# Keeping the slot masks of a graph kernel in DRAM, dropping a small store, moving a product to ScalarE, and smaller first batches

## The chip, the cores and the metric

The kernel runs on one core of a Trainium2 chip. The metric is the time of one execution on the device in microseconds (us). TensorE is called PE in the profile, VectorE DVE, ScalarE ACT, GpSimd POOL, SyncE SP. Transfers issued by SP stand in a queue of SP's own, which issues them in order; a transfer whose condition is not met holds up all behind it. [...]

## What is computed

Two graph layers over 6,250 nodes and 100,000 edges with 128 features each; the edges are sorted by their target node `dst`. Each layer is added to its input and normalized. Cut to what matters:

```python
# layer 0: two graph convolutions
deg  = segment_sum(ew, dst)                    # self-loops included
dinv = where(deg > 0, rsqrt(deg), 0)
h    = relu(segment_sum((x @ W1)[src] * norm[:, None], dst) + b1)
h    = segment_sum((h @ W2)[src] * norm[:, None], dst) + b2
x    = layernorm(x + sigmoid(h))
# layer 1: attention over the edges of a node
z  = x @ fc_w.T;  rh = edge_attr @ fc_r_w.T
e  = z[src] @ a0 + z[dst] @ a1 + rh @ a2
e  = where(e >= 0, e, 0.01 * e)
alpha = softmax of e over the edges of each dst
agg   = segment_sum(alpha[:, None] * (z[src] + rh), dst)
x  = layernorm(x + relu(agg + z @ loop_w))
```

## The kernel before

**Chunks and slots.** The edges are cut into 49 chunks (`NC`) of 2,048 (`CC`), each held as 128 partitions by 16 (`TC`). Since the edges are sorted by target, the targets of one chunk lie in a window of 144 nodes. The rows of the sources are gathered by matrix products with one-hot masks: the node table lies in SBUF as bf16 parts (`hot`), and each edge is given a slot, a group of 17 (`G`: 12 ordinary ones and 5 for spilled edges) and a place of 128 in that group. `sort()` (lines 688 to 787) works this out for three, then four, then seven chunks at a time: it ranks the edges, gets each edge's place `pm` and group `pg`, builds the two one-hot masks of a chunk, `ohm` (128x2048, place) and `ohg` (128x272, group), and brings the edges' data into slot order by the products of line 771. The slots' sources go to `srd` in DRAM, and from there come back spread over all partitions as `mask` rows (L849), are compared (L853) and stored for the later stages (`masks`, L854). The steps of `sort()` are dealt out between the chunks of the first convolution by `sort_to`.

**A chunk of a convolution.** `pick` (L467) gathers: 144 small products L476 into three PSUM tiles, copied with the slot's weight `swt` by ScalarE to `got` (L481), and five indirect loads by GpSimd for the spilled edges (`far`, L485). It builds the window mask `wm` on VectorE (L491, L498). `weigh` (L515) puts the weights on the spilled part of `wm` on ScalarE, `scatter` (L522) sums into the window on PE, and `add_in` (L527) adds the window to the accumulator. Scatter and addition of a chunk run one chunk later than its gather.

**The stages.** First convolution (L840 to L879), second convolution (L894 on, its order written out by hand), in which the attention scores of nodes `asd` are also worked out piece by piece with the layer's new node table (`x1_of`, L372; its bf16 parts are stored to `hz`, L426). Then comes the softmax stage (L1029 on), in which this change has most of its lines.

**The hand-over.** After the second convolution `asd` is stored to DRAM (L1019); only the branch for unusual graphs at the program's end reads that table, and it writes it itself first (L1407). Then `asd` is cut into bf16 parts `adp` (L1020 to L1023). `hot` is filled again from `hz` in four loads on ScalarE's queue (L1190).

**The softmax stage.** `scores()` (L1173) goes through batches of chunks: `ends` (scores of targets), `starts` (scores of sources, two halves per chunk: a row `rk` of 256 KB loaded on SP three ahead, L1054; compared on VectorE, L1087; 24 products L1094; `sel`, L1097; `asr`, L1098) and `softmax`. A chunk can only be summed once its batch is in `ready`. The batches hold 2, 5, then 7 chunks. While a batch is summed, the scores of the next are dealt out by `beside`. For each chunk, `shares` (L1196) brings the shares `al` to slot order: it builds `ohm` and `ohg` a second time (L1199, L1201) out of `pm` and `pg`, which stay in SBUF, multiplies (`put`, L1204), and sums in 16 products (L1208) and a reduction to `swt` (L1209). Then come `pick` and `scatter` as above, and `edge_part` (L1211): the edge features `et` are loaded in two halves (L1220), `ms` compares 16 segments with a window of 32 (L1225) and is multiplied by the shares `aw` (L1227), 16 products give `r` (L1238), ScalarE copies it (`sw`, L1243) and two products bring it to the window (L1249). `out_of` (L428) finishes blocks of nodes whose sums are complete.

**What sets the order.** Except in the second convolution, a scheduler sets the order of each engine's instructions and of each queue's transfers before the run, by its own estimate of when each is ready and by priority, which follows the order of the program text. Tiles come from pools with a set number of buffers (`bufs`); a tile's next use waits until the last reader of that buffer is done.

Of the kernel before, what the change touches and what calls it, by code (L numbers as in the profile page):

```python
# [10 lines left out]
BF16 = mybir.dt.bfloat16  # L11
I32 = mybir.dt.int32
AF = mybir.ActivationFunctionType
# [25 lines left out]
def gnn_kernel(ctx, tc, x, src, dst, ea, ew, W1, b1, W2, b2, fcw, fcrw, attn, loopw, out):  # L39
# [30 lines left out]
    while c0 < NC:  # L70
        n = min((2, 5)[len(batches)] if len(batches) < 2 else 7, NC - c0)
        batches.append((c0, n))
        c0 += n
# [31 lines left out]
    masks = dram.tile([NC, P, GP * P], BF16, name="masks")  # L105

# [82 lines left out]

    pm = keep.tile([P, NC, TC], BF16, name="pm")  # L190
    pg = keep.tile([P, NC, TC], BF16, name="pg")
# [495 lines left out]

    def sort():

        for c0, n in sorts:  # L690
# [61 lines left out]
            nc.vector.tensor_add(pm[:, some, :], r_, t_)  # L752
            nc.vector.scalar_tensor_tensor(t_, k_i[:, :n, :], float(GP), grp[:, some, :], op0=OP.add, op1=OP.subtract)
            nc.vector.tensor_mul(t_, t_, o)
            nc.vector.tensor_add(pg[:, some, :], grp[:, some, :], t_)
            slots = sp.tile([P, BATCH, NF], F32, name="slots")
            for c in cs:
                ohm = sp.tile([P, P, TC], BF16, name="ohm")
                nc.vector.tensor_tensor(ohm, iota_t, pm[:, c, None, :].to_broadcast([P, P, TC]), op=OP.is_equal)  # L759
                ohg = sp.tile([P, TC, G], BF16, name="ohg")  # L760
                nc.vector.tensor_tensor(ohg, iotab[:, None, :G].to_broadcast([P, TC, G]),
                                        pg[:, c, :, None].to_broadcast([P, TC, G]), op=OP.is_equal)
                put = sp.tile([P, TC, NF], BF16, name="put")
                nc.vector.tensor_tensor(put[:, :, : G * F].rearrange("p t (g f) -> p t g f", f=F),  # L764
                                        ohg[:, :, :, None].to_broadcast([P, TC, G, F]),
                                        rec[:, c, :, None, :].to_broadcast([P, TC, G, F]), op=OP.mult)
                nc.vector.tensor_tensor(put[:, :, G * F :], ohg[:, :, GP:],  # L767
                                        blk[:, c, :, None].to_broadcast([P, TC, GS]), op=OP.mult)
                ps = ps_c.tile([P, NF], F32, name="rec")
                for t in range(TC):  # L770
                    nc.tensor.matmul(ps, ohm[:, :, t], put[:, t, :], start=t == 0, stop=t == TC - 1)  # L771
                nc.scalar.copy(slots[:, c - c0, :], ps)
                yield
# [120 lines left out]
    with tc.tile_pool(name="conv2", bufs=2) as wp, tc.tile_pool(name="arp", bufs=2) as ap_, \  # L894
# [124 lines left out]
        nc.sync.dma_start(asd_d[:, :].rearrange("(b p) k -> p b k", p=P), asd)  # L1019
# [9 lines left out]
    with tc.tile_pool(name="look", bufs=2) as lp, tc.tile_pool(name="conv3", bufs=2) as wp, \  # L1029
# [20 lines left out]
        def sources(i):  # L1050

            if i < 2 * NC:
                rks[i] = lp.tile([P, HC], BF16, name="rk", bufs=3)
                nc.sync.dma_start(rks[i], srow[i // 2, None, i % 2 * HC : (i % 2 + 1) * HC].to_broadcast([P, HC]))  # L1054
# [129 lines left out]
        for i in range(2):  # L1184
            sources(i)
        steps = scores()
        next(steps)
# [7 lines left out]

        def shares(c, al3, i):  # L1196

            ohm = mp.tile([P, P, TC], BF16, name="ohm", bufs=1)
            nc.vector.tensor_tensor(ohm, iota_t, pm[:, c, None, :].to_broadcast([P, P, TC]), op=OP.is_equal)  # L1199
            ohg = mp.tile([P, TC, G], BF16, name="ohg", bufs=1)  # L1200
            nc.vector.tensor_tensor(ohg, iotab[:, None, :G].to_broadcast([P, TC, G]),  # L1201
                                    pg[:, c, :, None].to_broadcast([P, TC, G]), op=OP.is_equal)
# [8 lines left out]
        def edge_part(c, aw, i):  # L1211
# [15 lines left out]
            nc.vector.tensor_mul(ms, ms, aw[:, i, :, None].to_broadcast([P, NL, WS]))  # L1227
# [24 lines left out]
        pieces = Pieces(lambda b0, n: out_of(acc2, sum_r, b0, n, xp, ps_c, "rec"))  # L1252
        held = None
# [214 lines left out]
```

## Time and profile before

| | us |
|---|---|
| median of 3 runs | 2010.08 (2000.15 to 2014.5) |
| profiled execution | 2011.72, of which the span 2009.9 |
| first convolution, 49 chunks | 170 to 655 |
| second convolution, 49 chunks | 740 to 1205 |
| first batch ready in the softmax stage | about 1307 |
| `sw` copies of chunks 7, 35, 48 | 1438, 1847, 1985 |
| busy: PE, DVE, ACT, POOL | 1594.6, 1635.5, 945.4, 1102.0 |
| DMA: bytes, mean rate | 306.95 MB, 153 GB/s |

A row of the profile names the line, the engine, the operation, the written and the read tile, the count, and then the busy time and the mean duration in ns, followed by the idle time in front of such instructions and what ended it. Durations of neighbours on one engine overlap a little, so that a merged entry of twelve `got` takes 3.21 us though the mean of one is 0.38. "SPq" and "ACTq" rows are transfers being issued; their time is that of the issue, not of the transfer. A timeline row can merge neighbours of one kind ("x4").

### The profile page before, as it was taken

The page shows a single profiled execution, that of the slowest core. Times are in us where ns is not written, and L with a number is a line of the kernel's source. Part 1 is how long each engine was busy: PE and PEld are TensorE (multiplying, and loading weights), DVE is VectorE, ACT ScalarE, POOL GpSimd, SP SyncE. Part 2 cuts the span into 40 slices and gives each one's busy share as a digit, 9 for nine tenths or more (in the row PEclk, how much of TensorE's full clock was granted, in tenths as well). Part 3 has the DMA queues.
Part 4 walks back from the last instruction along what each step waited for, and adds up shares of the span by engine and source line. Part 5 has one row for each costly group of instructions (what it writes and reads, how often), then busy time and mean ns, then how long its engine had stood idle before and what let it go on. Part 6 is the DMA issues. An engine that isn't in the chain of part 4 may idle for free.

```text
span 2009.9 us, 78721 instructions
## 1 busy us (share of the span) xinstructions
PE 1594.6 (79%) x33767; PEld 1441.6 (72%) x33767; DVE 1635.5 (81%) x3252; ACT 945.4 (47%) x3098; POOL 1102.0 (55%) x953
## 2 busy tenths in 40 slices
PE   2877889988888868889888863368888888888996
PEld 2556878878877757778778752358877787877985
DVE  7787978988985348999989954689989999997773
ACT  1255445455455655577666743013433444434543
POOL 4026666777767348888888850214343434534772
PEclk9978989999999758899999985569999999999998
DMA  2115234244236247777777766655666666655662
GB/s 62 37 43 157 65 112 135 68 120 143 74 104 191 62 132 228 220 226 260 233 226 258 221 212 64 160 137 140 186 161 194 178 177 180 182 171 150 190 181 70
DMA packets 260881, 306.95 MB, mean 153 GB/s; under 512 B 44145, under 2 KB 199543, under 8 KB 253470
## 3 DMA queue, kind: packets, MB, share of 16 engines
q1 hardware_dynamic: 228915, 244.95, 40.0%
q0 software_dynamic: 23520, 48.22, 11.5%
q10 hardware_dynamic: 8088, 8.65, 1.4%
q8 instruction: 268, 4.39, 0.9%
q14 instruction: 90, 0.74, 0.1%
HBM read 260.42 MB, written 41.30 MB: 150 GB/s over the span
## 4 chain that ended last, share of the span: by engine, by line
PE 36%; DVE 36%; DMA 13%; issue 7%; ACT 6%; DVEq 1%; POOL 1%; SPq 0%; ACTq 0%; POOLq 0%
PE win L522 15%; PE g L476 7%; DVE wm L491 5%; DVE sel L1097 3%; DVE put L764 2%; DMA et<-in_edge_attr_dram 2%; DVE ohm L759 2%; PE rec L1208 2%; DVE et L980 2%; ACT got L481 2%; PE mm L333 2%; DMA mask<-srd 2%; DMA far<-g,sidx 2%; DMA mask<-masks 1%; DMA hz<-part 1%
## 5 line engine op out<-in xcount | busy, mean ns | idle before, releaser
L485 POOL DMA_INDIRECT far<-g,sidx x490 | 728.5, 1487 | 232.6 <-PE win L522 103.5
L481 ACT ACTIVATE got<-g,swt 128x128 f32<-128x128 f32 x1764 | 485.0, 382 | 373.5 <-PE g L476 170.3
L485 POOL DMA_INDIRECT far<-zd,sidx x245 | 309.9, 1265 | 459.0 <-PE win L522 332.3
L522 PE MATMUL win<-wm,got 128*128 128x144 f32 x3528 | 521.9, 305 | 11.6 <-issue 11.5
L522 PEld LDWEIGHTS win<-wm,got 128*128 128x128 f32 x3528 | 485.1, 204 | 29.4 <-issue 18.7
L476 PE MATMUL g<-hot,mask 128*32 128x128 bf16 x21168 | 392.8, 229 | 95.5 <-issue 55.3
L476 PEld LDWEIGHTS <-mask 128*32 128x32 bf16 x21168 | 336.3, 102 | 129.6 <-issue 93.2
L491 DVE TENSOR_TENSOR wm<-iota,sdst 128x1728 f32<-128x1728 f32 x147 | 286.7, 1950 | 3.9 <-DMA g<-rows 3.7
L515 ACT ACTIVATE wm<-wm,swt 128x64 f32<-128x64 f32 (+1 forms) x735 | 201.4, 356 | 80.6 <-DVE wm L498 46.2
L522 PE MATMUL win<-wm,far 128*128 128x64 f32 (+1 forms) x1470 | 187.0, 273 | 15.5 <-DMA far<-g,sidx 14.9
L522 PEld LDWEIGHTS win<-wm,far 128*128 128x128 f32 x1470 | 182.4, 194 | 16.9 <-issue 13.5
L1094 PE MATMUL k<-adp,rk 128*128 128x49 bf16 x2352 | 93.6, 196 | 64.5 <-DVE sel L1097 51.3
L1094 PEld LDWEIGHTS <-rk 128*128 128x128 bf16 x2352 | 86.0, 104 | 76.7 <-DVE rk L1087 40.9
L980 DVE TENSOR_TENSOR et<-et,ar_row 128x2048 f32<-128x2048 f32 (+1 forms) x49 | 111.6, 2279 | 25.9 <-DMA et<-in_edge_attr_dram 25.9
L527 DVE TENSOR_TENSOR acc<-acc,win 128x144 f32 x147 | 44.3, 302 | 99.4 <-PE win L522 86.8
L981 DVE TENSOR_REDUCE dots<-et 128x16 f32<-128x2048 f32 (+1 forms) x49 | 112.0, 2286 | 1.7
L322 POOL TENSOR_TENSOR hot<-low,hot 128x512 bf16<-128x512 f32 x24 | 32.5, 1355 | 141.1 <-DVE hot L321 101.6
L1097 DVE TENSOR_TENSOR sel<-k,ohb 128x392 f32<-128x392 f32 x98 | 84.0, 858 | 4.9 <-PE k L1094 4.6
L764 DVE TENSOR_TENSOR put<-ohg,rec 128x1360 bf16<-128x1360 bf16 x49 | 76.8, 1568 | 0.0
L717 ACT CAST own<-r 128x768 bf16<-128x768 f32 x49 | 39.3, 803 | 71.7 <-PE r L714 46.2
L771 PE MATMUL rec<-put,ohm 128*128 128x90 bf16 x784 | 59.1, 242 | 15.8 <-DVE put L767 14.9
L1087 DVE TENSOR_SCALAR rk<-rk,iotap 128x1024 bf16<-128x1024 bf16 x98 | 50.1, 511 | 26.5 <-DMA rk<-srow 26.5
(397 smaller groups left out, 2326.4 us busy)
## 6 DMA issues: line engine op xcount, KB each, us to landing
et<-in_edge_attr_dram SPq DMA_DIRECT2D x97, 512.0 KB
et<-in_edge_attr_dram SPq DMA_DIRECT2D x48, 1024.0 KB
mask<-masks SPq DMA_DIRECT2D x98, 384.0 KB
rk<-srow SPq DMA_DIRECT2D x98, 256.0 KB
mask<-srd SPq DMA_DIRECT2D x49, 384.0 KB
masks<-mask SPq DMA_DIRECT2D x49, 384.0 KB
far<-g,sidx POOLq DMA_INDIRECT x490
g<-rows SPq DMA_DIRECT2D x24, 256.0 KB
```

Source lines behind the costliest of these rows:

```text
L476: nc.tensor.matmul(ps[32 * q : 32 * q + 32, g, :], mask[:, (g0 + g) * P + 32 * q : (g0 + g) * P + 32 * q + 32], hot[:, 4 * (g0 + g) + q, k ...
L481: nc.scalar.activation(got[:, g, :], ps[:, g, :], AF.Copy, scale=swt[:, c, g0 + g : g0 + g + 1])
L485: nc.gpsimd.indirect_dma_start(out=got, out_offset=None, in_=table[:, :], in_offset=bass.IndirectOffsetOnAxis(ap=sidx[:, c, g : g + 1], ax ...
L491: nc.vector.tensor_tensor(wm[:, : GP * WC].rearrange("p (g w) -> p g w", w=WC), iota[:, None, 1 : WC + 1].to_broadcast([P, GP, WC]), sdst[ ...
L515: nc.scalar.activation(m, m, AF.Copy, scale=swt[:, c, g : g + 1])
L522: nc.tensor.matmul(ps[:, n0 : n0 + m.shape[-1]], rows[g], m, start=g == 0, stop=g == G - 1)
L764: nc.vector.tensor_tensor(put[:, :, : G * F].rearrange("p t (g f) -> p t g f", f=F), ohg[:, :, :, None].to_broadcast([P, TC, G, F]), rec[: ...
L771: nc.tensor.matmul(ps, ohm[:, :, t], put[:, t, :], start=t == 0, stop=t == TC - 1)
L980: nc.vector.tensor_mul(et[:n], et[:n], ar_row[:n, None, :].to_broadcast([n, TC, D]))
L981: nc.vector.tensor_reduce(dots[:n, c, :], et[:n], AX.X, OP.add)
L1094: nc.tensor.matmul(ps[:, s, :], mk[:, s * P : (s + 1) * P], adp[:, 0, k, :NB], start=k == 0, stop=k == 2)
L1097: nc.vector.tensor_mul(sel, ps, ohb.rearrange("p b s -> p s b"))
```

## The change

Six edits. The store of `asd` (old L1019) is left out. The first two `rk` rows and the first step of the scores are put under `tc.high_priority()`, so that the scheduler takes them ahead of others. `ohm` and `ohg` become the two parts of one tile `slot` (128 x 2,320 bf16), which `sort()` stores to the new DRAM table `slotd` as soon as it is built; `pm` and `pg` are now small tiles of the sort. In the softmax stage `shares` no longer builds the masks but takes them from a tile that was loaded from `slotd` (two buffers); it asks for the next chunk's at its start, and `load_slots(0)` stands before the loop. In `edge_part` the product of `ms` and `aw` becomes 16 activations on ScalarE, each 128x32 with the share as its scale. The batches hold 2, 3, 4, 5, then 7 chunks, nine in all where there were eight.

```diff
-        n = min((2, 5)[len(batches)] if len(batches) < 2 else 7, NC - c0)
+        n = min((2, 3, 4, 5)[len(batches)] if len(batches) < 4 else 7, NC - c0)
...
+    slotd = dram.tile([NC, P, P * TC + TC * G], BF16, name="slotd")
...
-    pm = keep.tile([P, NC, TC], BF16, name="pm")
-    pg = keep.tile([P, NC, TC], BF16, name="pg")
...
+    def slot_views(slot):
+        return (slot[:, : P * TC].rearrange("p (q t) -> p q t", t=TC),
+                slot[:, P * TC :].rearrange("p (t g) -> p t g", g=G))
...
-                ohm = sp.tile([P, P, TC], BF16, name="ohm")
-                nc.vector.tensor_tensor(ohm, iota_t, pm[:, c, None, :].to_broadcast([P, P, TC]), op=OP.is_equal)
-                ohg = sp.tile([P, TC, G], BF16, name="ohg")
+                slot = sp.tile([P, P * TC + TC * G], BF16, name="slot")
+                ohm, ohg = slot_views(slot)
+                nc.vector.tensor_tensor(ohm, iota_t, pm[:, c - c0, None, :].to_broadcast([P, P, TC]), op=OP.is_equal)
                 nc.vector.tensor_tensor(ohg, iotab[:, None, :G].to_broadcast([P, TC, G]),
-                                        pg[:, c, :, None].to_broadcast([P, TC, G]), op=OP.is_equal)
+                                        pg[:, c - c0, :, None].to_broadcast([P, TC, G]), op=OP.is_equal)
+                nc.sync.dma_start(slotd[c], slot)
...
-        nc.sync.dma_start(asd_d[:, :].rearrange("(b p) k -> p b k", p=P), asd)
...
-        for i in range(2):
-            sources(i)
-        steps = scores()
-        next(steps)
+        with tc.high_priority():
+            for i in range(2):
+                sources(i)
+            steps = scores()
+            next(steps)
...
+        slots_in = {}
+
+        def load_slots(c):
+            if c < NC:
+                slots_in[c] = mp.tile([P, P * TC + TC * G], BF16, name="slot", bufs=2)
+                nc.sync.dma_start(slots_in[c], slotd[c])
+
         def shares(c, al3, i):
-            ohm = mp.tile([P, P, TC], BF16, name="ohm", bufs=1)
-            nc.vector.tensor_tensor(ohm, iota_t, pm[:, c, None, :].to_broadcast([P, P, TC]), op=OP.is_equal)
-            ohg = mp.tile([P, TC, G], BF16, name="ohg", bufs=1)
-            nc.vector.tensor_tensor(ohg, iotab[:, None, :G].to_broadcast([P, TC, G]),
-                                    pg[:, c, :, None].to_broadcast([P, TC, G]), op=OP.is_equal)
+            ohm, ohg = slot_views(slots_in.pop(c))
+            load_slots(c + 1)
...
-            nc.vector.tensor_mul(ms, ms, aw[:, i, :, None].to_broadcast([P, NL, WS]))
+            for s in range(k):
+                nc.scalar.activation(ms[:, s, :], ms[:, s, :], AF.Copy, scale=aw[:, i, s : s + 1])
...
+        load_slots(0)
```

More of the change, by code (lines that the diff above doesn't have):

```diff
@@ L751, in sort @@
             nc.vector.tensor_mul(t_, t_, o)
-            nc.vector.tensor_add(pm[:, some, :], r_, t_)
+            pm = sp.tile([P, BATCH, TC], BF16, name="pm")
+            pg = sp.tile([P, BATCH, TC], BF16, name="pg")
+            nc.vector.tensor_add(pm[:, :n, :], r_, t_)
             nc.vector.scalar_tensor_tensor(t_, k_i[:, :n, :], float(GP), grp[:, some, :], op0=OP.add, op1=OP.subtract)
             nc.vector.tensor_mul(t_, t_, o)
-            nc.vector.tensor_add(pg[:, some, :], grp[:, some, :], t_)
+            nc.vector.tensor_add(pg[:, :n, :], grp[:, some, :], t_)
             slots = sp.tile([P, BATCH, NF], F32, name="slots")
             for c in cs:
-                ohm = sp.tile([P, P, TC], BF16, name="ohm")
-                nc.vector.tensor_tensor(ohm, iota_t, pm[:, c, None, :].to_broadcast([P, P, TC]), op=OP.is_equal)
-                ohg = sp.tile([P, TC, G], BF16, name="ohg")
+                slot = sp.tile([P, P * TC + TC * G], BF16, name="slot")
+                ohm, ohg = slot_views(slot)
+                nc.vector.tensor_tensor(ohm, iota_t, pm[:, c - c0, None, :].to_broadcast([P, P, TC]), op=OP.is_equal)
                 nc.vector.tensor_tensor(ohg, iotab[:, None, :G].to_broadcast([P, TC, G]),
-                                        pg[:, c, :, None].to_broadcast([P, TC, G]), op=OP.is_equal)
+                                        pg[:, c - c0, :, None].to_broadcast([P, TC, G]), op=OP.is_equal)
+                nc.sync.dma_start(slotd[c], slot)
                 put = sp.tile([P, TC, NF], BF16, name="put")
```

## The prediction

> **What bounds the kernel now.** I read the page's row of slices first, then the busy time by stages, then the timelines of the places where an engine stands idle. The stages are my cut: the first convolution (170 to 655 us), the second (740 to 1205), the hand-over to the softmax stage (1240 to 1310), that stage's first chunks (to 1438), its steady part (chunks 7 to 35) and its tail, where no scores are left to work out.
>
> ```profile
> DVE  7787978988985348999989954689989999997773
> ```
>
> VectorE (DVE) is at nine tenths for most of the span; the dips lie at 650 to 750 us and at 1205 to 1300. Busy time by stage (columns: stretch, length, then busy us and instructions of PE, PEld, DVE, ACT, POOL, granted clock, DMA share, GB/s):
>
> ```profile
> 170.00:655.00 485.00, 418.75 (x9258) 385.35 (x9260) 404.95 (x851) 249.81 (x862) 341.39 (x237) 0.93 0.41 120
> ...
> 1240.00:1310.00 70.00, 25.02 (x481) 22.38 (x480) 44.34 (x108) 3.74 (x10) 15.95 (x12) 0.51 0.86 128
> 1310.00:1438.00 128.00, 100.00 (x2226) 91.08 (x2227) 115.67 (x317) 40.59 (x148) 39.13 (x32) 0.84 0.56 147
> 1438.00:1847.00 409.00, 350.29 (x8150) 321.26 (x8154) 376.40 (x882) 165.15 (x559) 169.72 (x141) 0.96 0.63 175
> 1860.00:1985.00 125.00, 116.17 (x2816) 110.67 (x2805) 88.19 (x165) 64.56 (x233) 83.14 (x58) 1.00 0.65 173
> ```
>
> In the steady part DVE is busy 376.4 of 409 us (92%), TensorE (PE) 86%: DVE binds, PE is close behind. In the tail PE is at 93% and DVE at 71%: PE binds. One chunk takes 409/28 = 14.6 us in the first and 125/12 = 10.4 us in the second. In the hand-over nobody is busy. Its queue and DVE:
>
> ```profile
> 1238.82 0.37 SPq L1019 DMA_DIRECT2D asd_d<-asd  x1
> 1240.10 12.45 SPq L426 DMA_DIRECT2D hz<-part  x1
> ...
> 1255.56 5.84 SPq L1054 DMA_DIRECT2D rk<-srow  x1
> ```
> ```profile
> 1247.12 0.20 DVE L1078 TENSOR_TENSOR adg<-one,adg 128x48 f32<-128x48 f32 x1
> 1268.62 3.47 DVE L1087 TENSOR_SCALAR rk<-rk,iotap 128x1024 bf16<-128x1024 bf16 x1 [21.31 <-DMA rk<-srow]
> ```
>
> The store of the scores (L1019) is 49 x 128 = 6,272 pieces of 8 bytes. The next DMA behind it, a 96 KB store, needs 12.45 us only to be issued where its like takes 0.33; all that follows on that queue is late, and DVE waits 21.31 us for one row of `rk`. The durations that the sum needs, from the steady part:
>
> ```profile
> L481 ACT ACTIVATE got<-g,swt 128x128 f32<-128x128 f32 x336 | 93.1, 383 | 160.6 <-DVE swt L1209 111.8 <-PE win L522 39.1 <-DVE near L1073 5.4
> ...
> L1097 DVE TENSOR_TENSOR sel<-k,ohb 128x392 f32<-128x392 f32 x61 | 52.9, 868 | 1.4 <-PE k L1094 1.3
> ...
> L1199 DVE TENSOR_TENSOR ohm<-iota_t,pm 128x2048 bf16<-128x2048 bf16 x29 | 35.2, 1214 | 0.0
> ...
> L1227 DVE TENSOR_TENSOR ms<-ms,aw 128x512 f32<-128x512 f32 x28 | 18.9, 676 | 0.0
> ...
> L1201 DVE TENSOR_TENSOR ohg<-iotab,pg 128x272 bf16<-128x272 bf16 x30 | 13.0, 433 | 0.0
> ```
>
> **The change, part by part.** The profiled execution took 2011.7 us (span 2009.9 and 1.8 around it), 1.6 above the median of the runs, 2010.1.
>
> *The store goes.* What it held up is the 21.3 us wait and the stretched `rk` comparison behind it (3.47 us against the usual 0.48): 24.3 us at most. Next late are the transfers themselves: the last quarter of `hot` (1152 KB, landed 11.2 us after its issue at 1266.0 in the chain of waits), and the first two slot masks, which the new order puts among the `rk` rows on SP's queue. Each is 128 x 2,320 bf16 = 594 KB. I take 4 us off for that: **-20** (bounds -24 and -12). That the first `rk` rows and `dk` go ahead saves nothing more: the wait is for the fourth row, whose buffer is only free when PE has used the first, and until 1240 DVE waits for the chain of x1 pieces in any case. The place of L1037/L1038 behind them is free for the same reason.
>
> *Slot masks are loaded, not rebuilt; shares are multiplied on ScalarE.* DVE loses 1.214 + 0.433 + 0.676 = 2.32 us per chunk, 114 us in 49 chunks. What that is worth differs by stage.
> In the first chunks (0 to 6) DVE is at 90%: 7 x 2.32 x 0.9 = 14.6 us. The new batches ask scores of three chunks, not five, before chunk 2: four halves less by the fourth chunk in the new order, each 0.87 + 0.56 + 0.48 + 0.36 = 2.3 us, 9 us put off to where DVE has room. I take **-15** for both together (-24 to -8), since the first batch's softmax, whose chain is unchanged, still stands in front. The ninth softmax costs DVE some 8 us (its 25 small operations by their rows), under PE where DVE is no longer the bound; with that cover gone it is +8.
> In the steady part DVE comes to 13.4 - 2.3 = 11.1 us per chunk and PE, 350.3/28 = 12.5 us, binds. Filled as in the tail (93%) that is 13.45 us, or -32 in 28 chunks.
>
> ScalarE now bounds how well PE can be filled. The nearest row is the weighting of `wm`, also in place with a scale per partition, 128x64:
>
> ```profile
> 1874.78 0.35 ACT L515 ACTIVATE wm<-wm,swt 128x64 f32<-128x64 f32 x1 [3.88 <-DVE swt L1209]
> 1875.15 1.14 ACT L481 ACTIVATE got<-g,swt 128x128 f32<-128x128 f32 x4
> 1876.17 1.07 ACT L515 ACTIVATE wm<-wm,swt 128x64 f32<-128x64 f32 x4
> ```
>
> Four in 1.07 us, one alone 0.35: one every 0.24. The Trainium skill, "ScalarE: Activation LUTs", section "Rules for kernel authors", says to give a multiplication to VectorE, not to ScalarE, and its section on the cost of ACT_TABLE_LOAD gives 186 ns, 93 more for a scale held per partition, 0.833 ns per element, 93 ns of it overlapped: 0.213 us for 32 elements, 3.4 us for 16, where DVE took 0.68. By the row it is at most 16 x 0.24 = 3.8. I take 3.4, as these are half as wide. The rule alone would call this edit a loss of 2.7 us per chunk; the rows say that ScalarE had 8.7 us free per chunk in the steady part (5.9 busy of 14.6), so total time is no bound: 9.3 of 13.5, and 8.8 of 10.4 in the tail.
> Its order is. The new order on ScalarE in the tail is per chunk: 3 `wm`, 4 `got`, 14 `ms`, 8 `got`, 2 `ms`, 2 `wm`, `sw`. Behind the fourteen stand the last eight `got`, and the last two `ms`, for which the `r` products wait, and after them `sw`, L1249, the next one-hot products L1208 and `swt`, for which the next `wm` and `got` wait. That is a ring: `r` 1.1, `sw` with its hand-offs 0.8, L1249 0.8, L1208 1.2, `swt` 0.4, then 0.8 + 1.1 + 3.0 + 2.15 + 0.6 on ScalarE: 11.9 us, against 10.4 in the tail. Hand-offs are estimated from gaps of 0.2 to 0.3 in the timeline, so I take 11.5: **+13** in 12 chunks (0 to +18). In the steady part `sel` and `k` work adds about a microsecond and a half to the ring, 13.4, about PE's 13.45; the two will not mesh fully: 13.8, **-22** (-32 to 0).
>
> *Storing the masks in the first convolution.* 49 stores of 594 KB. In order, SP has seven stores in a row, then the `srd` store and the mask rows; the rows needed `srd` before too, so nothing new queues there except until the seventh comparison is done, which `srd` also needs. What is new: the comparison for chunk c+2 waits until the store of c has landed. In the trace the two pairs are built from 360.19, both `ohg` done at 365.80, and the third `ohm` starts at 369.64: 3.8 us. The Trainium skill, "DMA: Bandwidth & Descriptors", "Anatomy of one DMA", fits 2.0 us plus bytes/436e3: 3.4 us, no wait. By the trace, 1152 KB in 11.2 us amid traffic, it is 5.8: 2 us for each of 8 bursts, 16. The bursts fall into lulls of DMA (share 0.41 in the stage), so I am near the first: 4. Also, the first slot store is now ahead of the `degr` load on SP, which went out at 96.88; `ohg` is done only at 100.4, and the load is used at 106.93: +2. Together **+6** (0 to +20). No gain is possible, as nothing is taken out there.
>
> DMA in the steady part: SP's queue moved 41.2 MB in 24.2% of 485 us in the first stage, 2.85 us of all engines per MB, so 1.7 us per slot mask: the share goes from 0.63 to about 0.80 at 13.6 us per chunk. The second convolution ran at 0.73. Each slot load waits on SP until PE's L1208 of the chunk before last has freed its buffer, and `rk`, `et` and `mask` loads queue behind it. I cost that at nothing because all of these are asked for about a chunk ahead; without that cover, one late load of 3.4 to 5.8 us per chunk less the chunk's slack.
>
> Sum: -20 - 15 - 22 + 13 + 6 = **-38**: 2011.7 - 38 = 1973.7, and 1.6 less against the median: **1972 us**.
>
> **Rivals.**
> A (0.50), the above; its own range is 1950 to 1992.
> B (0.17), the ring doesn't close, since `ms` fits under PE's 93%: steady -32, tail 0, first stage 0, starts -24 and -16: -72, **1938**. For it: ScalarE stands idle 160.6 us before `got` alone. Against: fourteen activations sit in the middle of that order.
> C (0.18), DMA at 0.8 and the ring take the steady gain: 0 there, tail +13, first stage +16, starts -35: -6, **2004**. For it: the hand-over shows what a loaded queue does. E (0.04): the 21 us were not the store's, and come back under another name: 1992.
> D (0.11), slower: the ring of ScalarE binds everywhere. If an activation of 32 columns takes 0.35 us as the lone `wm` does, unoverlapped, 16 are 5.6, the ring 14.1 in the tail and 15.6 in the steady part: +45 + 28 - 35 + 6 = +44, **2054**. It decides from where the mean of those 40 chunks, now 13.3 us, exceeds 14.5. Against it: the four `wm` in 1.07 us.
>
> **The numbers.** About 1% (20 us) can be told from no change. Faster by more than that: A but for its upper edge and B, 0.65; within: C, E and A's edge, 0.24; slower: D, 0.11. The range leaves out D and half of B: 1935 to 2010.
>
> **What would show it.** The `hz` store issued in under 1 us and no DVE wait above 6 us near 1247; 13.8 us per chunk in the steady part with PE above 89%; in the tail `r` or `sw` waiting for `ms` on ScalarE and a pace of 11.5; in the first stage waits of `ohm` for slot stores of a few us. It is wrong if the `rk` wait stays, if the steady pace stays at 14.6, or if `put` or PE's L1208 waits for slot loads.

## The result and the profile after

| | before | changed |
|---|---|---|
| median (20 executions each, same chip) | 2007.64 us (1999.4 to 2023.25) | 2000.82 us (1990.85 to 2009.41) |
| ratio, 95% interval | | 0.9964 [0.9945, 0.9983] |
| profiled execution's span | 2009.9 us | 1998.6 us |
| DMA: bytes, mean rate | 306.95 MB, 153 GB/s | 365.18 MB, 183 GB/s |

The change is worth -7 us, where -38 was forecast. In a second measurement of the same kernel the ratio is 0.9982 [0.9963, 1.0002] (that measurement is called "again" below). A profiled execution can lie 10 us and more off its kernel's median, so I read two of the changed kernel: the first has a span of 1998.6 us, the second ("again") 1989.0.

VectorE's row of slices, changed kernel (compare it with the row at the start of the prediction):

```profile
DVE  7797979989986348899899955879988878775453
```

Each digit is the busy share of 50 us, in tenths. From about 1,450 us on its nines have become eights and sevens, and fives and less in the tail: the work did leave VectorE. The same windows of the changed kernel as were shown before, put where its stages lie (stretch, length, busy us and instructions of PE, PEld, DVE, ACT, POOL, granted clock, DMA share, GB/s):

```profile
170.00:655.00 485.00, 416.81 (x9376) 386.11 (x9377) 410.77 (x858) 252.47 (x879) 313.07 (x234) 0.93 0.55 172
...
1235.00:1285.00 50.00, 26.61 (x480) 22.37 (x480) 38.47 (x101) 7.35 (x27) 16.38 (x12) 0.54 0.67 201
1285.00:1418.00 133.00, 109.21 (x2390) 96.34 (x2393) 112.61 (x328) 64.54 (x262) 45.69 (x35) 0.87 0.62 183
1418.00:1832.00 414.00, 359.80 (x7999) 329.25 (x7991) 323.57 (x790) 261.54 (x1011) 168.48 (x136) 0.93 0.73 212
1844.00:1973.00 129.00, 118.34 (x2817) 110.64 (x2809) 65.31 (x132) 101.51 (x421) 77.03 (x58) 1.00 0.73 214
```

The hand-over fell from 70 to 50 us. In the steady part (chunks 7 to 35) VectorE is busy 323.6 us instead of 376.4, ScalarE 261.5 instead of 165.2, and the stretch is 414 us long instead of 409. PE is busy 87% of it (86% before): nothing that VectorE lost has turned into a fuller PE.

The issues of SP's queue in the hand-over, changed kernel:

```profile
1234.89 0.32 SPq L425 DMA_DIRECT2D hz<-part  x1
...
1238.75 0.57 SPq L1208 DMA_DIRECT2D slot<-slotd  x1
1239.86 2.45 SPq L1059 DMA_DIRECT2D rk<-srow  x2
1242.35 1.24 SPq L1208 DMA_DIRECT2D slot<-slotd  x1
1248.42 0.32 SPq L1059 DMA_DIRECT2D rk<-srow  x1
```

and VectorE's wait there:

```profile
1245.48 0.82 DVE L1092 TENSOR_SCALAR rk<-rk,iotap 128x1024 bf16<-128x1024 bf16 x1 [4.02 <-DMA rk<-srow]
```

Without 6,272 pieces in front of it the `hz` store is issued in 0.32 us, not 12.45, and the wait of 21.31 us is one of 4.02. What VectorE waits for in the steady part, first before, then changed (wait, us in total, times, longest):

```profile
DVE acc L527 <- PE win L522: 8.8, 12, 5.3
...
DVE rk L1087 <- DMA rk<-srow: 2.7, 2, 2.1
```
```profile
DVE acc L526 <- PE win L521: 34.9, 16, 6.1
DVE rk L1092 <- DMA rk<-srow: 24.5, 21, 3.4
```

VectorE now waits for PE, and for rows of `rk` that had been on time. By the starts of chunk copies (`sw`) the two profiled executions of the changed kernel compare with the one before, stage by stage, as follows. Below, "steady pace" is the time from chunk 7 to 35 over 28 chunks, "tail pace" that from chunk 35 to 48 over 13.

| stretch | before | changed | again | forecast | measured |
|---|---|---|---|---|---|
| start to `left` (both convolutions) | 1238.7 | 1233.4 | 1234.0 | +6 | -5, -5 |
| `left` to the first chunk | 68.9 | 49.6 | 49.9 | -20 | -19, -19 |
| chunks 0 to 7 | 130.5 | 135.6 | 133.2 | -15 | +5, +3 |
| chunks 7 to 35 | 409.2 | 413.9 | 404.0 | -22 | +5, -5 |
| chunks 35 to 48 (the tail) | 137.3 | 140.6 | 142.3 | +13 | +3, +5 |
| what is left | 25.3 | 25.5 | 25.5 | 0 | 0, 0 |

The store's gain came as forecast. The gain from relieving VectorE did not come at all. What kept it back is what the experiments were for.

### The profile page after: what moved, and what is told of

Read it like the earlier page. It is cut to its first block, busy times and chain, and to the rows that moved or that the text cites. A ratio compares the mean times of both kernels' runs of the same rounds, so it can differ in the third digit from the quotient of the medians.

```text
span 1998.6 us, 79601 instructions
## 1 busy us (share of the span) xinstructions
PE 1606.0 (80%) x33777; PEld 1447.0 (72%) x33777; DVE 1549.6 (78%) x3131; ACT 1106.2 (55%) x3882; POOL 1076.7 (54%) x953
## 2 busy tenths in 40 slices
DMA packets 268780, 365.18 MB, mean 183 GB/s; under 512 B 39487, under 2 KB 194889, under 8 KB 261360
## 4 chain that ended last, share of the span: by engine, by line
PE 36%; DVE 30%; DMA 13%; ACT 10%; issue 8%; DVEq 1%; POOL 1%; SPq 0%; ACTq 0%; POOLq 0%
PE win L521 16%; PE g L475 6%; DVE wm L490 5%; DMA rk<-srow 4%; ACT got L480 3%; DVE put L770 2%; DVE et L986 2%; DVE sel L1102 2%; PE mm L332 2%; DMA far<-g,sidx 2%; PE k L1099 2%; PE r L1250 2%; DVE slot L765 2%; ACT ms L1239 2%; PE rec L1219 2%
## 5 line engine op out<-in xcount | busy, mean ns | idle before, releaser
L484 POOL DMA_INDIRECT far<-g,sidx x490 | 702.3, 1433 | 256.6 <-PE win L521 105.5
L475 PE MATMUL g<-hot,mask 128*32 128x128 bf16 x21168 | 403.4, 229 | 93.9 <-issue 62.0
L475 PEld LDWEIGHTS <-mask 128*32 128x32 bf16 x21168 | 341.7, 101 | 127.9 <-issue 95.8
L1239 ACT ACTIVATE ms<-ms,aw 128x32 f32<-128x32 f32 x782 | 176.7, 318 | 51.3 <-DVE ms L1236 47.8
L521 PE MATMUL win<-wm,far 128*128 128x64 f32 (+1 forms) x1470 | 184.6, 271 | 15.2 <-DMA far<-g,sidx 12.7
L1102 DVE TENSOR_TENSOR sel<-k,ohb 128x392 f32<-128x392 f32 x98 | 83.7, 854 | 10.6 <-PE k L1099 10.2
L1250 PE MATMUL r<-et,ms 128*32 128x128 f32 x1564 | 77.1, 279 | 3.9 <-ACT ms L1239 3.5
L770 DVE TENSOR_TENSOR put<-slot,rec 128x1360 bf16<-128x1360 bf16 x49 | 76.6, 1563 | 0.0
```

The costliest lines, as they stand in the source:

```text
L475: nc.tensor.matmul(ps[32 * q : 32 * q + 32, g, :], mask[:, (g0 + g) * P + 32 * q : (g0 + g) * P + 32 * q + 32], hot[:, 4 * (g0 + g) + q, k ...
L484: nc.gpsimd.indirect_dma_start(out=got, out_offset=None, in_=table[:, :], in_offset=bass.IndirectOffsetOnAxis(ap=sidx[:, c, g : g + 1], ax ...
L521: nc.tensor.matmul(ps[:, n0 : n0 + m.shape[-1]], rows[g], m, start=g == 0, stop=g == G - 1)
L1102: nc.vector.tensor_mul(sel, ps, ohb.rearrange("p b s -> p s b"))
L1239: nc.scalar.activation(ms[:, s, :], ms[:, s, :], AF.Copy, scale=aw[:, i, s : s + 1])
L1250: nc.tensor.matmul(ps[WS * q : WS * q + WS, g, :], ms[:p, s, :], ets[g][:p, s % 8, :], start=half == 0, stop=half == 1 or s + 1 == k)
```

## The experiments

Three theories at first. *Queue*: the loads of the slot masks (594 KB each) stand on SP's queue between the `rk` rows and make them late. *Ring*: ScalarE's 16 activations, in its fixed order, hold up PE. *PE*: PE's own work at the granted clock, with a fill that does not improve, is the bound.

**First job: one part at a time.** It ran on another chip, on which the kernel before takes 2375.38 us, so only ratios and paces within the job can be compared.

The kernel before without its store:

```diff
-        nc.sync.dma_start(asd_d[:, :].rearrange("(b p) k -> p b k", p=P), asd)
```


> The kernel before with the store of the scores left out and nothing else changed. All theories: the wait of 21 us in the hand-over goes, -17 to -24 us, ratio about 0.990. If so, the rest of the change together costs about 13 us. If the ratio is 0.996 or more, the store was not what the wait cost (the next transfers take its place).

The changed kernel with its masks rebuilt on VectorE (nothing is stored to `slotd` or loaded from it):

```diff
-            ohm, ohg = slot_views(slots_in.pop(c))
-            load_slots(c + 1)
+            ohm = mp.tile([P, P, TC], BF16, name="ohm", bufs=1)
+            nc.vector.tensor_tensor(ohm, iota_t, pm[:, c, None, :].to_broadcast([P, P, TC]), op=OP.is_equal)
...
```


> The changed kernel, but with the slot masks rebuilt on VectorE as before; neither stored nor loaded. Queue theory (the loads of slot masks on SP's queue make the rk rows late, and that eats the steady part's gain): rk waits in the steady part fall from 24.5 us to under 6, VectorE is at 90% again, pace 14.2 to 14.5 us per chunk, ratio 0.990. Ring theory (sixteen activations in ScalarE's order set the pace): pace stays at 14.8 or rises, since VectorE's work is in the ring too; ratio 0.995 to 1.005. PE theory (PE's own work at the granted clock leaves no room): pace 14.8.

The changed kernel with the edge products on VectorE:

```diff
-            for s in range(k):
-                nc.scalar.activation(ms[:, s, :], ms[:, s, :], AF.Copy, scale=aw[:, i, s : s + 1])
+            nc.vector.tensor_mul(ms, ms, aw[:, i, :, None].to_broadcast([P, NL, WS]))
```


> The changed kernel, but with the product of ms and aw on VectorE again. Ring theory: steady pace from 14.8 to about 13.8 us per chunk and the tail from 10.8 to 10.4, 25 to 30 us in all, ratio 0.982. Queue theory: rk waits stay at 20 us or more and the pace at 14.5 to 14.8; the tail alone may gain 5 us, ratio 0.992 to 0.996.

The changed kernel with four `rk` buffers instead of three, and rows asked for half a chunk earlier (to make room, `sw` is left one buffer, and the small row `zero` shares a tile):

```diff
-                rks[i] = lp.tile([P, HC], BF16, name="rk", bufs=3)
+                rks[i] = lp.tile([P, HC], BF16, name="rk", bufs=4)
...
-                sources(2 * c + h + 2)
+                sources(2 * c + h + 3)
...
-        for i in range(2):
+        for i in range(3):
```


> The changed kernel with four buffers for the rk rows instead of three, loaded three ahead instead of two (room for it: one buffer less for the sw tile, and the small zero row shares a tile). Queue theory: rk waits in the steady part fall from 24.5 us to under 8 and the pace from 14.8 to about 13.9, ratio 0.985. Ring theory and PE theory: rk waits fall too, but the pace stays within 0.2 of 14.8, ratio 0.995 to 0.998.

| | ratio, 95% interval | steady pace, us per chunk | tail pace |
|---|---|---|---|
| store only | 0.9899 [0.9838, 0.9959] | 17.78 | 13.9 |
| masks rebuilt | 0.9886 [0.9850, 0.9922] | 17.78 | 13.5 |
| products on VectorE | 0.9920 [0.9891, 0.9949] | 17.09 | 14.3 |
| four `rk` | 0.9830 [0.9767, 0.9892] | 17.09 | 14.1 |

Taking out the store alone already gives a gain of the size that all four show. No single undoing of the rest stands out: four buffers look best, but their interval overlaps the others. The changed kernel itself was not measured on this chip.

**Second job**, on a chip where the kernel before takes 2004.83 us. The changed kernel again:

> The changed kernel as it is, so that it stands on the same chip as the three runs below. If this chip is like the first one (the kernel before at about 2008 us), 0.996 and a steady pace of 14.8 us per chunk; if it is like the second one (2375 us), all theories that put the rest of the change at a net loss of about 0.6% expect 0.995 or so, worse than the 0.990 of the store alone; if the change stands at 0.988 to 0.990 here, the rest of it nets nothing.

With the slot masks loaded from GpSimd's queue:

```diff
-                nc.sync.dma_start(slots_in[c], slotd[c])
+                nc.gpsimd.dma_start(slots_in[c], slotd[c])
```


> The changed kernel with the slot masks loaded from GpSimd's queue, no longer between the rk rows on SP's. Queue theory (an rk row waits on SP behind a slot load): the waits of DVE for rk fall from some 24 us in the steady part to under 5, the steady pace to about 14.0 and the ratio to about 0.985. Bandwidth[...]: the rk waits stay, or go over to the slot or mask loads, and the time is that of the changed kernel. PE theory: rk waits fall and the pace stays within 0.2 us of the changed kernel's.

With four `rk` buffers and the edge products on VectorE (both edits above):

> Four rk buffers, so that a row is asked for half a chunk earlier, and the edge masks times shares again on VectorE. If both the late rows and ScalarE's order cost time, this gains more than four buffers alone did (0.983): about 0.978. If only the rows do, it is 0.983 to 0.988, since VectorE gets 0.68 us per chunk back. If PE binds, 0.983.

The kernel before without its store, with four `rk` buffers:

> The kernel before without its store of the scores, and with four rk buffers; masks, products and batches as before. If four buffers help because the slot loads make rows late (queue theory), there are none here, rows are on time, and this equals the store alone: 0.990. If they help in the start (the fourth row no longer waits for PE to use the first) it is about 0.985, as good as the changed kernel with four buffers, and the masks and products are worth nothing.

Measured: changed again 0.9982 [0.9963, 1.0002]; GpSimd's queue 1.0013 [0.9991, 1.0035]; four `rk` with products on VectorE 0.9876 [0.9817, 0.9935]; store only with four `rk` 0.9886 [0.9817, 0.9956]. The last two can't be told apart, nor from the store alone in the first job (0.9899): masks from DRAM add nothing that shows.

The *queue* theory falls. VectorE's waits in the steady part with the slot loads on GpSimd's queue:

```profile
DVE acc L526 <- PE win L521: 38.6, 17, 6.1
DVE rk L1092 <- DMA rk<-srow: 24.1, 18, 4.0
```

The rows are as late as before (24.5), though no slot load stands in front of them any more. Which queue asks makes no difference to that wait. The pace is 14.95. Nor is it the load on DMA alone: in the run with half of `win` below the same loads run at a DMA share of 0.78, more than in the changed kernel, and VectorE waits only 9.2 us for rows. SP's queue stands for PE to free the buffer of a row 41.1 us in the steady part, about as long as before the change (43.3). What makes the rows late stays open.

**Third job: what is worth what.** The kernel before takes 2004.95 us. The batches undone:

```diff
-        n = min((2, 3, 4, 5)[len(batches)] if len(batches) < 4 else 7, NC - c0)
+        n = min((2, 5)[len(batches)] if len(batches) < 2 else 7, NC - c0)
```


> The changed kernel with the batches 2, 5, then 7, as before. In the changed kernel chunks 0 to 7 took 133 to 136 us against 130 before, where 15 less was forecast. If the batches are the cause (one softmax more in front, smaller ones), this stretch falls to about 120 to 125 us and the ratio to 0.990. If the slot loads and late rk rows are, it stays at 133 to 140 and the ratio at 0.996 to 0.998.

No `rk` loads (the scores are then those of other nodes; the comparisons and products run as before):

```diff
-                nc.sync.dma_start(rks[i], srow[i // 2, None, i % 2 * HC : (i % 2 + 1) * HC].to_broadcast([P, HC]))
...
-                nc.vector.tensor_scalar(mk, mk, iotap, None, op0=OP.is_equal)
+                nc.vector.tensor_scalar(mk, iota_t.rearrange("p q t -> p (q t)")[:, :HC], iotap, None, op0=OP.is_equal)
```


> The changed kernel without the loads of the rk rows: the comparison reads a constant tile of the same shape, so the scores are those of other nodes; all other work stands. Late rows (theory: slot loads take the 16 engines when VectorE asks for rows): the 20 to 25 us of rk waits go, PE waits less for sel, and the steady pace falls from 14.4 to 14.8 to about 13.8, the time by 25 us or more (0.985). PE theory (PE's 12.0 us per chunk at full speed, 12.8 at the granted clock, and 2 us of small waits that do not depend on VectorE): the pace stays within 0.2 us.

Half of the near `win` products left out of the softmax stage, in the changed kernel, and in the kernel with the store removed and four `rk`:

```diff
+    def scatter(held, ps_w, every=1):
...
         for g in range(G):
+            if g < GP and g % every:
+                continue
...
-                    win = scatter(held, ps_w)
+                    win = scatter(held, ps_w, 2)
```


> The changed kernel with every second of the twelve near products into win left out in the softmax stage, some 1.8 us of PE per chunk; all that feeds them still runs. PE theory: the steady pace falls by 1.5 to 1.8 us, and 49 chunks by about 80 us (0.958). Late rows or VectorE as the bound: by less than 0.6 us in the steady part (the tail still gains), 30 to 40 us in all.

> The same products left out of the kernel before without its store, with four rk buffers, where VectorE still rebuilds the masks (13.4 us of 14.6 per chunk). If VectorE bound the steady part before, as the prediction had it, the pace falls only to about 14.0 (0.6 us) and less than in the changed kernel. If PE bound it already before, it falls by as much as in the changed kernel, 1.2 us or more.

Measured: batches undone 1.0038 [1.0017, 1.006]; no `rk` loads 0.9887 [0.983, 0.9943]; half `win` 0.9779 [0.9735, 0.9823] in the changed kernel, 0.9819 [0.9753, 0.9885] in the other.

*Late rows* are a part, not the whole. The steady part without `rk` loads, and that of the changed kernel again:

```profile
1410.70:1811.90 401.20, 352.03 (x8105) 324.12 (x8103) 323.12 (x791) 260.18 (x1008) 171.20 (x139) 0.96 0.62 181
```
```profile
1417.00:1821.00 404.00, 351.62 (x7998) 322.32 (x7996) 323.33 (x790) 261.06 (x1011) 173.48 (x137) 0.96 0.74 218
```

At the same granted clock, 0.96, the part takes 401 us instead of 404, a pace of 14.33 where 13.8 was expected of late rows. Another 5 us are gained in chunks 0 to 7 (128.6 against 133.2). The medians differ by more, 22 us, and against the first trace of the changed kernel, at clock 0.93, the steady part is 12.7 us shorter; so what late rows cost is known only to lie between these figures (the run also moves less data, at a DMA share of 0.62). But with no row to wait for, the pace is still half a microsecond over the forecast, and VectorE then waits 42.8 us for `win` instead.

*PE and VectorE were close to a tie, and the change left PE in front.* The pair with half of `win` shows it. The steady part of the changed kernel with half `win` (with all of it: the row of 404 us above); then that of the store-only kernel with four `rk`, first with all of `win`, then with half:

```profile
1419.80:1802.30 382.50, 329.09 (x7648) 288.47 (x7646) 319.17 (x789) 257.56 (x1004) 166.57 (x137) 0.96 0.78 228
```
```profile
1414.90:1825.40 410.50, 356.26 (x8153) 329.06 (x8149) 376.05 (x879) 164.08 (x557) 174.04 (x141) 0.94 0.64 173
1409.40:1811.90 402.50, 321.95 (x7706) 292.23 (x7707) 375.77 (x885) 161.95 (x555) 177.61 (x138) 0.89 0.65 176
```

Both have the same products left out, 1.4 to 1.6 us of PE per chunk (the row of these products has 96.4 us in "again" and 101.7 in the first trace, and 56.2 with half of them). In the changed kernel PE's busy time falls by 22.5 us at the same clock, 0.96, and the stretch by 21.5: the time follows PE. In the other PE's busy time falls by 34.3 us and the stretch by only 8.0, with VectorE busy 93% of it. The clock is lower there (0.89 against 0.94), but PE stands idle for 80 us even so. The ratios agree: 0.9982 to 0.9779 in the changed kernel, 0.9886 to 0.9819 in the other, with some 12 to 15 us of the gain in the tail in both. So VectorE did limit the old order, and does not limit the changed one.

*And ScalarE hands its masks to PE one by one.* In the changed kernel PE lost 40.2 us of `win` at the same clock, but only 22.5 us of busy time in all. The group of the `r` products, which read the edge masks, in the steady part of three kernels (busy us, mean ns, then the idle time in front): the kernel before, the changed kernel, the changed kernel with half `win`:

```profile
L1238 PE MATMUL r<-et,ms 128*32 128x128 f32 x896 | 31.9, 275 | 2.1 <-DVE ms L1227 2.0
```
```profile
L1250 PE MATMUL r<-et,ms 128*32 128x128 f32 x896 | 41.2, 276 | 0.4 <-ACT ms L1239 0.4
```
```profile
L1252 PE MATMUL r<-et,ms 128*32 128x128 f32 x896 | 70.3, 285 | 6.0 <-ACT ms L1241 4.8 <-issue 1.2
```

The same 896 products, each as long as before (275 to 285 ns), are in flight for 31.9, 41.2 and 70.3 us. When all masks of a chunk are ready, its 32 products take 1.08 us together. When ScalarE hands the masks over one by one, PE takes the products one by one, with other products between them and in part over them. So the 29.1 us more that this group has with half of `win` are not all lost to PE: by PE's total, some 18 of the 40 us came back. That it was `r` that took them back is likely, since PE waits 4.8 us for `ms` in front of it, but no run leaves out half of `win` with the products on VectorE. With the products on VectorE and four `rk` the group is at 30.6 again.

**Fourth job: what the rest of the change nets.** The kernel before takes 2005.45 us. The store alone, and four `rk` in the changed kernel, both as in the first job:

> The kernel before without its store, nothing else, on a chip where the kernel before takes about 2005 us. If the rest of the change nets a loss of about 0.8%, as the slow chip had it, this gives 0.988 to 0.991. If the rest nets nothing, it gives 0.996 to 0.998, the changed kernel's own ratio.

> The changed kernel with four rk buffers, on this chip. If the gain on the slow chip (0.983 against 0.990 for the store alone) holds, 0.983 to 0.986, the best of all. If it was that chip's, 0.990 to 0.993: 7 us less in the hand-over than the changed kernel, and no more.

The new batches in the kernel without its store and with four `rk`; and the changed kernel with another share-out of PSUM:

```diff
-            tc.tile_pool(name="ps_g3", bufs=3, space=PSUM) as ps_g, tc.tile_pool(name="ps_w3", bufs=1, space=PSUM) as ps_w, \
-            tc.tile_pool(name="ps_r3", bufs=1, space=PSUM) as ps_r, tc.tile_pool(name="ps_k3", bufs=1, space=PSUM) as ps_k, \
+            tc.tile_pool(name="ps_g3", bufs=2, space=PSUM) as ps_g, tc.tile_pool(name="ps_w3", bufs=1, space=PSUM) as ps_w, \
+            tc.tile_pool(name="ps_r3", bufs=1, space=PSUM) as ps_r, tc.tile_pool(name="ps_k3", bufs=2, space=PSUM) as ps_k, \
```


> The kernel before without its store, with four rk buffers and with the new batches 2 to 5, then 7. Undoing the batches cost the changed kernel 0.56%. If that is the batches' own worth, this gives 0.983 (0.9886 less 0.56%). If they only help where VectorE has been relieved of the masks, it is 0.989 or more.

> The changed kernel with two banks for the score products k and two for g instead of one and three, so that PE need not wait until VectorE has read the last k (14 to 18 us of the 54 that PE idles in the steady part). If PE's idle time there is a sum of such hand-offs, the steady pace falls by 0.3 to 0.5 us and the ratio to 0.990 to 0.993. If the wait only goes over to the next product on PE, the pace stays within 0.2 us; it becomes worse if g needs its third bank.

| | ratio, 95% interval | chunks 0 to 7, us | steady pace (clock) | tail pace |
|---|---|---|---|---|
| store only | 0.9916 [0.9888, 0.9945] | 131.5 | 14.50 (0.97) | 10.6 |
| changed, four `rk` | 0.9929 [0.9905, 0.9953] | 130.9 | 14.58 (0.95) | 11.1 |
| store only, four `rk`, new batches | 0.9973 [0.9949, 0.9996] | 151.5 | 14.63 (0.94) | 10.3 |
| changed, two `k` banks | 0.9970 [0.9941, 0.9999] | 136.3 | 14.64 (0.96) | 11.1 |

The store alone is worth -0.84%, 17 us: more than the whole change, at 0.9964 and 0.9982 in other jobs (the intervals meet at 0.9945 and no further). So all the rest of it nets a loss of about 0.5 to 0.7%, 10 to 13 us. By stages, the changed kernel is longer than this one in the hand-over (49.6 and 49.9 us against 47.3, so that the rows put ahead by priority bring nothing to be seen), in chunks 0 to 7 (135.6 and 133.2 against 131.5) and in the tail (140.6 and 142.3 against 137.6). The same steady part, store only:

```profile
1414.20:1820.30 406.10, 348.57 (x8164) 320.51 (x8163) 376.90 (x883) 164.96 (x560) 169.38 (x141) 0.97 0.63 176
```

406 us with VectorE busy 377 us, against 404 (at 0.96) and 414 (at 0.93) with VectorE busy 323: 53 us less on an engine that is busy 93% of the time bought at most 2 at about the same clock.

Two banks for `k` move PE's wait for `sel` away and bring another: `k` waits 17.7 us for the comparison of `rk` (2.1 to 3.8 with one bank), and the pace stays. PE's idle time in the steady part (the stretch less PE's busy time) is 49 to 67 us in the kernel before, the changed one and all variants with their full products on this kind of chip, and is made of many waits, most under 3 us.

By the ratios of two jobs each, the new batches cost the store-only kernel with four `rk` 0.9% (chunks 0 to 7 take 151.5 us instead of 130.3), and are worth 0.6% in the changed kernel, none of it in chunks 0 to 7 (132.9 without them, 133.2 with them); the steady part is longer without them (424 us at clock 0.93, against 414 at the same). Part of why is in the next section; the rest is open.

No kernel that does the whole computation is faster than the store alone (0.9916) beyond its interval: store only with four `rk` has 0.9886, four `rk` with products on VectorE 0.9876, four `rk` in the changed kernel 0.9929, and their intervals overlap. The store alone is a single line taken out.

## Why the prediction was wrong

**The store, -20: right.** Measured -19 in both traces, with the wait that remains where it was put (4 us for the transfers), and -17 us by the ratio of the store alone. Rival E falls.

**The steady part, -22: the step that failed.** "PE, 350.3/28 = 12.5 us, binds. Filled as in the tail (93%) that is 13.45 us." That PE would bind was right; that VectorE's relief would fill it as the tail does was not. PE stayed at 87%, with 54 us of the 414 idle and 52 of the 404, and the pace at 14.8 and 14.4, where 13.8 was forecast. The tail has no scores to work out. In the steady part PE's queue passes through `dk`, `k` and the chain of softmax products, and in its fixed order waits a little at each for an answer from VectorE or ScalarE. The waits of PE there, first before, then changed:

```profile
PE rec L1208 <- DVE put L1204: 12.6, 14, 1.7
PE g L476 <- issue: 10.7, 8, 2.8
PE k L1094 <- DVE sel L1097: 6.9, 12, 1.1
PE k L1094 <- DVE rk L1087: 5.3, 9, 1.5
...
PE rec L1249 <- ACT sw L1243: 4.2, 9, 1.0
```
```profile
PE k L1099 <- DVE sel L1102: 14.2, 19, 1.8
PE rec L1261 <- ACT sw L1255: 8.1, 13, 2.6
...
PE rec L1129 <- DVE part L1146: 3.6, 4, 1.5
PE rec L1168 <- DVE e L1165: 3.0, 2, 2.1
```

The relief did take one wait away: that for `put` fell to 0.7 us. But PE's idle time in front of products of the scores, summed over their rows, rose from 24.9 of 59 us to 34.7 of 54 (39.3 of 52 in "again"). Without it, the changed kernel's PE is idle 0.7 and 0.5 us per chunk, no more than in the tail (0.9). That is where the fill was lost. Which of these waits would have to go to shorten the stretch is not shown: taking away the one for `sel` brought another.

Two things came on top. VectorE's answers became later by its own waits for rows (24.5 us, from 2.7). And the 12.5 us were read at a clock of 0.96 in one trace: busy time times clock is 350.3 x 0.96 = 336 before, 359.8 x 0.93 = 335 in the changed kernel, 351.6 x 0.96 = 338 again, so the same work lasts 10 us longer at 0.93; the two traces of one kernel differ by just that, and it is no effect of the change. By the same figures the longer time of the `r` group added nothing to PE's work.

Rival C came nearest (2004), with a steady part that gains nothing, but in part by luck: its +16 in the first stage was -5, its -35 for the starts was -14 to -16, and these misses cancel. Nor is its reason shown: DMA stood at 0.73, not 0.8, since the pace did not fall (0.73 of 14.8 us is the same 10.8 us per chunk as 0.80 of 13.6); rows were late, but undoing only that leaves a pace of 14.3.

I costed the queue of slot loads "at nothing because all of these are asked for about a chunk ahead". For `put`, which reads the slots, that held: 0 us of waits. For the `rk` rows it did not, but by the run on GpSimd's queue it was not the place in the queue that made them late.

**First chunks, -15: wrong, +3 to +5.** The prediction had "four halves less by the fourth chunk", their work "put off to where DVE has room". By chunk 7 they had come back with interest. Counts within chunks 0 to 7, first of the kernel before, then of the changed one:

```profile
L1097 DVE TENSOR_TENSOR sel<-k,ohb 128x392 f32<-128x392 f32 x22 | 18.7, 851 | 2.0 <-PE k L1094 2.0
...
L1159 DVE RECIPROCAL full<-full 82x128 f32<-82x128 f32 (+1 forms) x2 | 1.9, 940 | 0.0
```
```profile
L1102 DVE TENSOR_TENSOR sel<-k,ohb 128x392 f32<-128x392 f32 x25 | 21.3, 853 | 3.9 <-PE k L1099 3.9
...
L1164 DVE RECIPROCAL full<-full 50x128 f32<-50x128 f32 (+2 forms) x3 | 2.8, 938 | 0.0
```

Three more halves of scores (3 x 2.3 us by the prediction's own rows) and a third softmax (8 us) fall into this stretch: 15 of the 16 us of work that VectorE was to be spared. Its busy time in chunks 0 to 7 is 118.0 us before and 115.2 changed. The ninth softmax had been put "under PE where DVE is no longer the bound"; the batches' sizes say that it lies in the first chunks, where VectorE is at 85 to 90%. The kernel without the relief shows the price bare: 21 us. But these counts are not the whole cause. With the old batches in the changed kernel VectorE is busy only 107.5 us there, 81% of the stretch, and the stretch takes 132.9 us all the same; 10.0 us of that are waits for `rk` rows (0.8 before). So the other assumption of this term, that 0.9 of the work taken off VectorE is gained, fails here even without the new batches.

**Tail, +13: right in sign, +3 and +5.** The price of an activation held: 14 in 3.07 us, 0.219 each, against the estimate of 0.213 worked out from the Trainium skill, "ScalarE: Activation LUTs", section on the cost of ACT_TABLE_LOAD. The ring did not. The changed kernel's ScalarE in the tail, two chunks:

```profile
1846.90 0.83 ACT L514 ACTIVATE wm<-wm,swt 128x64 f32<-128x64 f32 x3 [2.12 <-DVE swt L1220]
1847.63 1.11 ACT L480 ACTIVATE got<-g,swt 128x128 f32<-128x128 f32 x4
1848.63 3.07 ACT L1239 ACTIVATE ms<-ms,aw 128x32 f32<-128x32 f32 x14
1851.60 2.13 ACT L480 ACTIVATE got<-g,swt 128x128 f32<-128x128 f32 x8
1853.59 0.56 ACT L1239 ACTIVATE ms<-ms,aw 128x32 f32<-128x32 f32 x2
...
1857.37 2.23 ACT L1239 ACTIVATE ms<-ms,aw 128x32 f32<-128x32 f32 x10 [2.19 <-DVE ms L1236]
1859.51 1.11 ACT L480 ACTIVATE got<-g,swt 128x128 f32<-128x128 f32 x4
```

The first is the order that the ring was built on, with each duration as forecast. In the second, ten activations run before the chunk's `got`, in the time in which ScalarE would wait for `swt`. The order differs from chunk to chunk; I had taken one chunk's for all. The pace is 10.8 to 11.0, from 10.56, not 11.5. Rival D falls by the same rows.

The rule of the Trainium skill against this edit ("ScalarE: Activation LUTs", "Rules for kernel authors") had been set aside because ScalarE had time to spare. It had. But nothing was gained either: with four `rk`, products on VectorE give 0.9876 [0.9817, 0.9935] and on ScalarE 0.9929 [0.9905, 0.9953]. The intervals overlap and come from two jobs, so that neither a loss nor a gain is shown in the time; that PE's `r` products are spread by it is shown.

**Storing the masks, +6: nothing to be seen.** Up to `left` it took 5 us less in both traces; in the other variants 0 to 17 us less where the masks are stored, and 3 us less to 2 more where they are not. VectorE's longest wait before building a mask in the first convolution is 1.4 us, and that was for PE: no mask waited for a store. The 3.4 us that the prediction gave a store rest on a fit that the section of the Trainium skill ("DMA: Bandwidth & Descriptors", "Anatomy of one DMA — SWDGE (gpsimd) path") states for transfers issued by GpSimd; these were issued by SP, and no run here shows how long one took to land. (The other figure, 5.8 us, comes to 5.6 with both sizes in the profile's KB, 580 and 1152.) Why the stretch is rather shorter with them stays open.

## What to carry to other kernels

When two engines stand within a few per cent of each other in a stretch, work taken off the busier one is not worth its own length; ask first how full the next one gets there. Take that fill from the same stretch, not from one with a simpler dependency chain. A product moved to an idle engine still changes when its results arrive: one instruction that delivers 16 masks at once and 16 that deliver them one by one are different to whoever reads them.

When smaller batches start a pipeline earlier, count what must be done by a fixed later chunk, not only by the first.

An edit with several parts should be measured with its parts alone: here one deleted line gave more than the whole.

## What the runs showed of the hardware

- A store of 6,272 pieces of 8 bytes cost 19 us by the hold on its queue alone, the next issue lasting 12.45 us instead of 0.32, though nobody read what it stored.
- The 32 products of 32 columns that a chunk has in `r` took 1.08 us together when their operands were ready at once. Fed one mask at a time, every 0.22 us, they were in flight for 70.3/28 = 2.5 us, other products between and over them.
- Putting the 16 MB of loads of the steady part on another queue left the rows of `rk` as late as before (24.1 against 24.5 us).
- One kernel took 2375 us on one chip and 2005 us on another; on either, granted clocks of the steady part varied by 0.03 to 0.04 between executions of kernels with all their products, which is worth some 10 us in the steady part, as much as several of the effects looked for.
